# An adaLN block with a gated delta rule: balanced join products, q norms from turned rows, and a table position for every side step

## The chip, the cores and the metric

The kernel runs on one core of one Trainium2 chip, in one launch. The metric is device time in microseconds of the whole program. A profiled execution is one run with the hardware profiler on; its "span" reaches from the first to the last instruction that the profile shows. In the text TensorE is PE, VectorE is DVE, ScalarE is ACT, GpSimd is POOL and SyncE, which issues nearly all DMAs, is SP. Each of them works through its own instructions in order and waits, where it must, on semaphores that another engine or a DMA raises.

## What is computed

Input `x` has 8 sequences of 512 rows and 256 channels. Modulation vectors come from `silu(c) @ wmod`. Then, in float32 throughout:

```python
h = layernorm(x) * (1 + ca) + sa
x = x + ga * attn(h)
h = layernorm(x) * (1 + cb) + sb
x = x + gb * ffn(h)          # top 2 of 6 experts, chosen per sequence

def attn(h):                 # 16 key heads, 32 value heads, all of width 128
    qkvz = h @ W_qkvz.T      # q, k, v, z
    q, k, v = silu(conv4(qkv))              # causal depthwise convolution, 4 taps
    beta, g = sigmoid(b), -exp(A_log) * softplus(a + dt_bias)
    # chunked delta rule
    A = -strict_tril((k * beta) @ k.T * decay)
    T = inverse(I - A)       # a triangular inverse for each chunk
    u = T @ (v * beta), ...  # v_new = u - (T k beta exp(g)) @ state
    out = (q exp(g)) @ state + tril(q @ k.T * decay) @ v_new
    state = state * exp(g_last) + (k exp(g_last - g)).T @ v_new
    return (rmsnorm(out) * norm_weight * silu(z)) @ W_out.T
```

`q` and `k` are divided by their norms over the 128 channels. The kernel works in chunks of 128 rows (4 per sequence) where the reference has 64; the mathematics is the same.

## The kernel before

**Pairs and turns.** The work is cut into 128 "pairs": 8 sequences times 16 key heads; a pair holds one key head and its two value heads. For each pair, over a hundred small steps (`step[name]`) are defined, each of which issues the instructions of one engine, sometimes several DMAs. A table `PLACE` gives every step a position. The step of pair n stands at `n * 1000 + PLACE[name]`; `TURN = 1000`. All steps of all pairs are sorted by this position and issued in that order, under `tc.manual_schedule()`, so the order on each engine is the order of the table. Since positions run from -600 to 13049, about 14 pairs are in flight at once, and in the middle of the run each turn issues the same sequence of steps, one of every name, each of another pair. A position says only in which order things are queued: an engine starts the next instruction as soon as its semaphores allow.

**What the steps are.** `pk`, `pq`, `pv0`, `pv1`, `pz0`, `pz1` project (PE, 128x512 outputs); `ck`, `ck1` to `ck3` and the like are the four taps of the convolution (the first on ACT, three on DVE); `sk`, `sq`, `sv0`, `sv1` are the SiLUs (ACT). `kt` turns k on PE into PSUM, `kn0` and `kn1` take squares with row sums of it (ACT), `kp` the root (POOL), `ks` the scalars (DVE). For q, `qq` squares on POOL in channel-by-row form, `ssq` sums over channels by four matmuls against a column of ones, `qc` copies the result (DVE), `qp` and `qs` finish. `kk0`, `kk1` are the products of keys with keys and queries, `dr0`, `dr1`, `de` the decays (ACT), `mt*`, `qk*` (DVE) and `md*`, `sd*` (POOL) mask and decay them. `mo`, `so*`, `ko`, `qo` write to DRAM; `in0`, `in1`, `jd`, `jc` bring things back in another layout.

**The triangular inverse.** For every fourth pair, 32x32 diagonal blocks of four pairs lie one matrix to a lane, and DVE inverts them in twenty parts that are spread over four turns as `lane0` to `lane4` (lines 831 to 916). The blocks are then joined to 64 and to 128 by PE products: `jw` makes the first product of both joins (lines 968 and 970, outputs in PSUM partitions 0 to 63 and 64 to 127), ACT copies (`jwa`, `jwb`), `jy` makes the second product (lines 990, 991 and 997), ACT copies (`jya`, `jyb`). The join to 64 belongs to pair n, the join to 128 to pair n - 1. Line 991 makes the transposed form of the 64-join that the 128-join needs as its `x6`.

**The chunk steps.** `pk1`..`pq3` multiply by the state, `r*` (DVE) the residual, `u*` (PE) applies the inverse, `wd*` (DVE) and `w*` (ACT) scale, `ds*` (PE) and `st*` (DVE) make the next state, `i*` (PE) and `o*` (DVE) the output, `sq0`..`sq3` (ACT), `rm` (DVE), `rp`, `sc0`, `sc1` (POOL) the RMS norm, `ot*`, `gt*`, `op*` turn, gate and project out.

**PSUM.** All PE outputs but the sums of the projection out come from one pool of six banks. A PE step that takes a bank waits for the last reader of that bank's earlier content, so an ACT or DVE step that is late can hold up a PE step that has nothing else to do with it.

**Side steps.** Once per sequence come `before_attention` (layer norm, gates, decay sums: 29 steps) and `after_attention` (second norm, choice of experts, loads of their weights, FFN: 45 steps). In the kernel before they stand at a regular distance: the lines that place them are

```python
order.append((at + 20 * TURN, lambda b=b: gates(b)))
if b:
    order.append((at - 5 * TURN - TURN // 2, lambda b=b: load_rows(b)))
    for k, fn in enumerate(before_attention(b)):
        order.append((at - 5 * TURN + 3 * TURN * k // 20, fn))
for k, fn in enumerate(after_attention(b)):
    order.append((at + 28 * TURN + TURN // 2 + TURN * k // 5, fn))
```

with `at = 16 * b * TURN`.

Of the kernel before, what the change touches and what calls it, by code (L numbers as in the profile page):

```python
# [22 lines left out]

TURN = 1000
PLACE = {
    "wk": -600, "pk": -547, "ck": -460, "ck1": -393, "pq": -382, "gb": -377, "ck2": -361, "ck3": -303,
    "cq": -282, "sk": -168, "cq1": -109, "cq2": -103, "cq3": -38, "kt": 50, "sq": 83, "kn0": 89,
    "kra": 221, "kn1": 225, "qq": 280, "kp": 290, "dr1": 291, "kk0": 294, "ssq": 311, "dr0": 320,
    "ks": 329, "kk1": 372, "qk0": 385, "mt0": 394, "qc": 397, "qk1": 406, "mt1": 433, "de": 469,
    "qo": 501, "md0": 502, "ko": 556, "sd0": 641, "so0": 675, "md1": 708, "mo": 716, "sd1": 729,  # L30
    "so1": 1144, "qp": 1244, "qs": 1781, "tl": 4319, "lane0": 4503, "lane1": 4583, "lane2": 4627,
    "lane3": 4678, "lane4": 4704, "wv": 6947, "lx": 7757, "ly": 7904, "pv1": 7948, "cv1": 8064,
    "pv0": 8175, "cv11": 8201, "cv12": 8276, "cv13": 8314, "cv0": 8316, "sv1": 8357, "cv01": 8398,
    "cv02": 8454, "jd": 8458, "cv03": 8508, "jw": 8589, "sv0": 8603, "jwa": 8629, "jwb": 8688,
    "jy": 8744, "jya": 8835, "jyb": 8900, "vt0": 8977, "jc": 8982, "vt1": 9015, "vr0": 9101,
    "vr1": 9119, "in0": 9637, "in1": 9670, "u0": 9932, "wd0": 9966, "w0": 10062, "ds0": 10127,
    "st0": 10137, "pk1": 10297, "r1": 10350, "i0": 10386, "u1": 10392, "o0": 10432, "wd1": 10450,
    "ds1": 10495, "w1": 10549, "st1": 10613, "pq1": 10683, "pk2": 10700, "tm1": 10719, "r2": 10724,
    "pq2": 10765, "tm2": 10863, "u2": 10907, "i1": 10925, "wd2": 10939, "o1": 10972, "w2": 11006,
    "ds2": 11017, "st2": 11136, "sq0": 11170, "i2": 11200, "wz": 11202, "o2": 11296, "pk3": 11322,  # L40
    "r3": 11353, "u3": 11396, "pq3": 11462, "w3": 11518, "sq1": 11538, "i3": 11541, "tm3": 11554,
    "sq2": 11574, "o3": 11619, "sq3": 11714, "pz1": 11731, "sz1": 11785, "pz0": 11813, "rm": 11878,
    "rp": 11940, "sz0": 11994, "sc0": 12039, "sc1": 12051, "ot0": 12154, "ot1": 12163, "gt0": 12243,
    "gt1": 12277, "op0": 12366, "op1": 12477, "xa0": 12865, "xa1": 13049,
# [31 lines left out]
def adaln_block(  # L76
# [91 lines left out]
    def norm_transposed(b, shift, scale, name):  # L168
# [42 lines left out]
        steps = [*[lambda c=c: stats(c) for c in range(NC)], deviations, roots]  # L211
        for kt in range(NKT):
            steps += [
                lambda kt=kt: scaled(kt, 0), lambda kt=kt: scaled(kt, 1),
                lambda kt=kt: turned(kt), lambda kt=kt: shifted(kt),
            ]
        return steps

    def before_attention(b):
# [81 lines left out]
        def g_leaves():  # L301
            d["gfar"] = gfar.tile([P, P], F32, name=f"gfar_{b}", tag="gfar")
            nc.sync.dma_start(d["gfar"], t["gt"])

        return [
            *norm_transposed(b, 0, 2, "a"), betas, sigmoid, biased, soft, soft_exp, ratio,
            lambda: series(15, 13, 11, 9), lambda: series(7, 5, 3), soft_end,
            decay_sums, decay_exp, decay_rest, g_turned, g_copy, g_leaves,
        ]

    def after_attention(b):
# [46 lines left out]
        def experts():  # L358
            s1 = f["s1"] = tiny("w1", [P, NKT, 2 * DFF])
            s2 = f["s2"] = tiny("w2", [P, NF, DM])  # L360
            v1 = f["v1"] = tiny("b1", [P, NF])
            v2 = f["v2"] = tiny("b2", [P, 2, DM])
            for k in range(2):
                e = nc.sync.value_load(f["ix"][0:1, k : k + 1], min_val=0, max_val=NE - 1)
                nc.sync.dma_start(
                    s1[:, :, k * DFF : (k + 1) * DFF],
                    w1[bass.ds(e, 1)].rearrange("e (kt p) f -> p (e kt) f", p=P),
                )
                for at, t, q, n in hidden_parts(k, 0, DFF):
                    nc.sync.dma_start(  # L370
                        s2[q : q + n, t, :], w2[bass.ds(e, 1), at : at + n, :].rearrange("e p m -> (e p) m")
                    )
                for half in range(2):
                    for at, t, q, n in hidden_parts(k, half * FP, FP):
                        at -= half * FP
                        nc.sync.dma_start(
                            v1[q : q + n, t : t + 1],
                            b1[bass.ds(e, 1), at : at + n, half : half + 1].rearrange(
                                "e p t -> p (e t)"
                            ),  # L380
                        )
                nc.sync.dma_start(
                    v2[:, k, :], b2[bass.ds(e, 1)].to_broadcast([P, DM])
                )
# [14 lines left out]
        def hidden(i, t):  # L399
            ps = f["ps", t] = bank(f"f1_{b}_{i}_{t}")  # L400
            for kt in range(NKT):
                mm(
                    ps[: MF[t], : 2 * P], f["s1"][:, kt, t * P : t * P + MF[t]],
                    d["hb"][:, kt, 2 * i * P : (2 * i + 2) * P], start=kt == 0, stop=kt == NKT - 1,
                )

        def gelu(i, t):
            if t == 0:
                f["hid"] = row.tile([P, NF, 2 * P], F32, name=f"hid_{b}_{i}", tag="hid", bufs=1)
            nc.scalar.activation(  # L410
                f["hid"][: MF[t], t, :], f["ps", t][: MF[t], : 2 * P], AF.Gelu,
                bias=f["v1"][: MF[t], t : t + 1],
            )

        def result(i):
            ps = f["f2"] = bank(f"f2_{b}_{i}")
            for c2 in range(2):
                for t in range(NF):
                    mm(
                        ps[:, c2 * DM : (c2 + 1) * DM], f["hid"][: MF[t], t, c2 * P : (c2 + 1) * P],  # L420
# [3 lines left out]
        def result_rows(i):  # L424
            o = f["o"] = row.tile([P, 2, DM], F32, name=f"of_{b}_{i}", tag="of", bufs=1)
            nc.vector.tensor_add(
                o, f["f2"].rearrange("p (c m) -> p c m", m=DM), bc_mid(f["v2"][:, 0, :], 2)
            )

        def result_gated(i):  # L430
            nc.vector.tensor_mul(f["o"], f["o"], bc_mid(d["gb"], 2))

        def result_added(i):
            nc.vector.tensor_add(f["o"], f["o"], d["x"][:, 2 * i : 2 * i + 2, :])

        def result_leaves(i):
            nc.sync.dma_start(
                out[b, 2 * i * P : (2 * i + 2) * P, :].rearrange("(c p) d -> p c d", p=P), f["o"]
            )

        steps = [
            *norm_transposed(b, 4, 6, "b"), column_sums, logits, choose, choice_exp, shares, spread,
            spread_copy, experts, weigh,
        ]
        for i in range(2):
            for t in range(NF):
                steps.append(lambda i=i, t=t: hidden(i, t))
                steps.append(lambda i=i, t=t: gelu(i, t))
            for fn in (result, result_rows, result_gated, result_added, result_leaves):
                steps.append(lambda i=i, fn=fn: fn(i))  # L450
# [50 lines left out]
    for step in before_attention(0):  # L501
        step()
# [10 lines left out]
    with ExitStack() as st:  # L513
# [162 lines left out]
        def q_squares(n, d):  # L676
            q = d["kqa"][:, :, 1, :]
            d["sq"] = w1b.tile([P, NC, P], F32, name=f"sq_{n}", tag="sq")
            nc.gpsimd.tensor_tensor(d["sq"], q, q, ALU.mult)  # L679

        def q_sums(n, d):
            ps = d["ssq"] = bank(f"ssq_{n}")
            for c in range(NC):
                mm(ps[:, c : c + 1], d["sq"][:, c, :], ones[:, 0:1], start=True, stop=True)  # L684

        def q_copy(n, d):
            d["nrm"] = sm.tile([P, NC], F32, name=f"nrm_{n}", tag="nrm")
            nc.vector.tensor_copy(d["nrm"], d["ssq"][:, :NC])  # L688
# [106 lines left out]
        add("qq", q_squares)  # L795
        add("ssq", q_sums)
        add("qc", q_copy)
# [184 lines left out]
        def join_y(n, d):  # L982
# [3 lines left out]
            for u in range(8):  # L986
                us = slice(64 * u, 64 * u + 64)
                if n < NPAIR:
                    y = d["y"]
                    mm(p5[:64, us], w5[:, u, :], halves(y[:, u, :]), start=True, stop=True)  # L990
                    mm(
                        p5[64:, 32 * u : 32 * u + 32], y[:, u, 0:64], w5[:, u, 0:32],
                        start=True, stop=True,
                    )
                if n > 0:
                    y = its[n - 1]["y"]
                    mm(p6[:64, us], w6[:, u, :], y[:, u, 64:128], start=True, stop=True)

        def join_y_128(n, d):
            if n > 0:  # L1000
                nc.scalar.copy(its[n - 1]["y"][0:64, :, 64:128], of_u(d["p6"], 64)[0:64])

        def join_y_64(n, d):
            if n < NPAIR:
                y, v = d["y"], of_u(d["p5"], 64)
                nc.scalar.copy(x6[32:64, :, 0:32], of_u(d["p5"], 32)[96:128])
# [3 lines left out]
        joins = ("jw", "jwa", "jwb", "jy", "jya", "jyb")  # L1010
        for name, fn in zip(joins, (join_w, join_w_128, join_w_64, join_y, join_y_128, join_y_64)):
# [261 lines left out]
        for b in range(NB):  # L1273
            at = HK * b * TURN
            order.append((at + 20 * TURN, lambda b=b: gates(b)))
            if b:
                order.append((at - 5 * TURN - TURN // 2, lambda b=b: load_rows(b)))
# [50 lines left out]
```

## Time and profile before

| what | value |
|---|---|
| median of 3 runs | 4172.03 us (4171.61 to 4175.54) |
| the profiled execution's own time | 4170.47 us |
| span of the profiled execution | 4168.8 us |
| mean granted PE clock | 0.984 |
| PE / DVE / ACT / POOL busy | 4006.1 / 3521.5 / 3180.3 / 1619.1 us |
| PE instructions | 27184 |

The profiled execution's time is 1.7 us over its span and 1.6 us under the median. A float32 matmul or its weight load appears as two PE instructions where the program has one; a transpose appears once. A busy time counts an instruction from its start to its modelled end, so PE's busy share includes the overlap of one matmul's end with the next one's start; distances from start to start say what an instruction costs in a stream. The profile's granted clock is 0.9 or more of full speed in all but the first slices of the span.

### The profile page before, as it was taken

The page shows a single profiled execution, that of the slowest core. Times are in us where ns is not written, and L with a number is a line of the kernel's source. Part 1 is how long each engine was busy: PE and PEld are TensorE (multiplying, and loading weights), DVE is VectorE, ACT ScalarE, POOL GpSimd, SP SyncE. Part 2 cuts the span into 40 slices and gives each one's busy share as a digit, 9 for nine tenths or more (in the row PEclk, how much of TensorE's full clock was granted, in tenths as well). Part 3 has the DMA queues.
Part 4 walks back from the last instruction along what each step waited for, and adds up shares of the span by engine and source line. Part 5 has one row for each costly group of instructions (what it writes and reads, how often), then busy time and mean ns, then how long its engine had stood idle before and what let it go on. Part 6 is the DMA issues. An engine that isn't in the chain of part 4 may idle for free.

```text
span 4168.8 us, 84578 instructions
## 1 busy us (share of the span) xinstructions
PE 4006.1 (96%) x27184; PEld 2968.0 (71%) x27184; DVE 3521.5 (84%) x7974; ACT 3180.3 (76%) x8946; POOL 1619.1 (39%) x1576
## 2 busy tenths in 40 slices
PE   6689999999999999999999999999999999999997
PEld 4467777777777777777777777777777777777776
DVE  4888888988899888898889888889888988889754
ACT  4578777778777787778877788777887778777663
POOL 4443444334443434433343434443434434444211
PEclk7799999999999999999999999999999999999999
DMA  4676666666666666656667566665667666666441
GB/s 122 158 191 169 175 174 185 171 165 171 176 174 162 177 166 180 180 147 175 176 176 182 160 166 175 175 176 166 167 169 183 169 165 175 172 169 178 131 115 49
DMA packets 1101605, 689.37 MB, mean 165 GB/s; under 512 B 667368, under 2 KB 964712, under 8 KB 1101168
## 3 DMA queue, kind: packets, MB, share of 16 engines
q1 hardware_dynamic: 1100352, 682.14, 61.3%
q8 instruction: 222, 3.64, 0.4%
q14 instruction: 215, 1.76, 0.1%
q10 hardware_dynamic: 816, 1.84, 0.1%
HBM read 435.68 MB, written 248.00 MB: 164 GB/s over the span
## 4 chain that ended last, share of the span: by engine, by line
PE 83%; DVE 10%; ACT 2%; DMA 2%; SPq 2%; issue 1%; POOL 0%; POOLq 0%; ACTq 0%; DVEq 0%
PE prv L590 10%; PE acc L1232 9%; PE prz L1187 9%; PE kk L722 6%; PE in L1140 5%; PE prk L590 5%; PE u L1096 5%; PE prq L590 4%; PE pk L1066 4%; PE pq L1071 4%; PE dst L1118 4%; PE ot L1213 3%; PE ssq L684 3%; PE vt L1022 2%; PE w L968 2%; PE py L990 2%
## 5 line engine op out<-in xcount | busy, mean ns | idle before, releaser
L1203 POOL TENSOR_TENSOR msq<-msq,mhalf 128x8 f32<-128x8 f32 x128 | 210.6, 1646 | 1216.2 <-DVE msq L1197 1216.2
L745 POOL TENSOR_TENSOR mta<-mta,dca 128x512 f32<-128x512 f32 x256 | 339.4, 1326 | 657.1 <-DVE nrm L688 391.1
L606 DVE SCALAR_TENSOR_TENSOR cvv<-prv,cw,cvv 128x511 f32<-128x511 f32 (+2 forms) x768 | 566.6, 738 | 0.4
L1111 ACT ACTIVATE w<-u,kept 128x128 f32<-128x128 f32 x1024 | 317.8, 365 | 317.9 <-PE u L1096 198.4
L590 PE MATMUL prv<-ha,wv 128*128 128x512 f32 x1024 | 488.2, 599 | 11.7 <-ACT jk L652 6.0
L1232 PE MATMUL acc<-wo,z 128*128 128x256 f32 x2048 | 484.1, 379 | 0.5 <-DVE z L1219 0.5
L1187 PE MATMUL prz<-ha,wz 128*128 128x512 f32 x1024 | 481.6, 593 | 2.8 <-DVE nrm L695 2.8
L1232 PEld LDWEIGHTS acc<-wo,z 128*128 128x128 f32 x2048 | 388.8, 190 | 61.0 <-issue 7.7
L752 POOL TENSOR_TENSOR dca<-qkm,dca 128x256 f32<-128x256 f32 x512 | 399.5, 801 | 20.1
L1140 PEld LDWEIGHTS in<-w,s 128*128 128x128 f32 x2048 | 298.8, 191 | 73.4 <-issue 39.0
L1103 DVE TENSOR_TENSOR wd<-u,kept 128x256 f32<-128x256 f32 x384 | 160.3, 418 | 218.0 <-PE u L1096 217.2
L707 ACT ACTIVATE dca<-gb,G 128x128 f32<-128x128 f32 x1024 | 328.3, 413 | 4.8 <-DMA sfar<-dca 4.8
L1162 ACT ACTIVATE jo<-o 128x128 f32<-128x128 f32 x1024 | 310.3, 313 | 6.6 <-DVE o L1153 3.2
L1140 PE MATMUL in<-w,s 128*128 128x128 f32 x2048 | 312.5, 275 | 0.0
L606 DVE SCALAR_TENSOR_TENSOR cvk<-prk,cw,cvk 128x511 f32<-128x511 f32 (+2 forms) x384 | 283.3, 738 | 15.9 <-ACT cvk L602 15.6
L1187 PEld LDWEIGHTS prz<-ha,wz 128*128 128x128 f32 x1024 | 193.9, 190 | 140.0 <-issue 123.1
L606 DVE SCALAR_TENSOR_TENSOR cvq<-prq,cw,cvq 128x511 f32<-128x511 f32 (+2 forms) x384 | 285.4, 743 | 4.9
L722 PE MATMUL kk<-kqa 128*128 128x256 f32 x1024 | 279.4, 397 | 6.0 <-ACT kqa L619 6.0
L679 POOL TENSOR_TENSOR sq<-kqa 128x512 f32<-128x512 f32 x128 | 133.2, 1041 | 377.8 <-ACT kqa L619 377.8
L590 PEld LDWEIGHTS prv<-ha,wv 128*128 128x128 f32 x1024 | 176.0, 192 | 140.3 <-issue 124.3
L1029 DVE TENSOR_TENSOR vr<-vt,kept 128x512 f32<-128x512 f32 x256 | 164.6, 685 | 128.8 <-PE vt L1022 128.8
L990 PEld LDWEIGHTS py<-y,w 128*64 128x64 f32 x2048 | 200.8, 138 | 100.2 <-issue 75.8
(211 smaller groups left out, 11143.6 us busy)
## 6 DMA issues: line engine op xcount, KB each, us to landing
gb<-gfar SPq DMA_DIRECT2D x128, 512.0 KB, 9.2
qfar<-kqa SPq DMA_DIRECT2D x128, 512.0 KB, 2.7
sfar<-dca SPq DMA_DIRECT2D x256, 256.0 KB, 3.6
s<-sfar SPq DMA_DIRECT2D x256, 256.0 KB, 4.5
wk<-in_dram SPq DMA_DIRECT2D x256, 128.0 KB, 3.4
kfar<-kra SPq DMA_DIRECT2D x128, 256.0 KB, 3.1
wv<-in_dram SPq DMA_DIRECT2D x128, 256.0 KB, 3.6
kq<-qfar SPq DMA_DIRECT2D x128, 256.0 KB, 3.7
```

Of the source, the lines that this page charges most:

```text
L590: mm(ps, d[wname][:, kt, j * P : (j + 1) * P], hT[:, kt, :], start=kt == 0, stop=kt == NKT - 1,)
L606: nc.vector.scalar_tensor_tensor(a[:, s:], ps[:, : SEQ - s], cw[:, ch, 3 - s : 4 - s], a[:, s:], ALU.mult, ALU.add)
L707: nc.scalar.activation(dc[:, c, h, :], d["gb"][:, 2 * gr + c, h * P : (h + 1) * P], AF.Relu, bias=rows[b]["G"][:, 2 * gr + c, k : k + 1], ...
L722: mm(ps[:, c2 * 2 * P : (c2 + 1) * 2 * P], d["kqa"][:, c, 0, :], d["kqa"][:, c].rearrange("p k i -> p (k i)"), start=True, stop=True,)
L745: nc.gpsimd.tensor_tensor(mt, mt, d["dc", gr].rearrange("p c h i -> p (c h) i"), ALU.mult)
L752: nc.gpsimd.tensor_tensor(dc, bc_mid(d["qkm", gr][:, c, :], 2), dc, ALU.mult)
L990: mm(p5[:64, us], w5[:, u, :], halves(y[:, u, :]), start=True, stop=True)
L1111: nc.scalar.activation(w[:, h, :], d["u", c][:, h * P : (h + 1) * P], AF.Copy, scale=d["br2"][:, c, h : h + 1],)
L1140: mm(ps[:, h * P : (h + 1) * P], d["s", c, h], d["w", c][:, h, :], start=True, stop=True,)
L1162: nc.scalar.activation(junk, d["o", c // 2][:, c % 2, h, :], AF.Square, accum_out=d["msq"][:, c, h : h + 1],)
L1187: mm(ps, d["wz"][:, kt, h * P : (h + 1) * P], rows[n // HK]["ha"][:, kt, :], start=kt == 0, stop=kt == NKT - 1,)
L1232: mm(ps[:, k * DM : (k + 1) * DM], d["z", h][:, c * P : (c + 1) * P], d["wo"][:, h, :], start=False, stop=p == HK - 1 and k == 1 and h == 1,)
```

## The change

It does four things.

1. In `jy`, line 991 is dropped, and the product of the 128-join (line 997) is written to PSUM partitions 64 to 127 instead of 0 to 63, so that two products per block remain, one for each column half. The transposed form is made by a new DVE step `jx` that transposes 32x32 blocks out of PSUM into `x6`; ACT's copy into `x6` is dropped from `jyb`.
2. The norm of q: `qq` (POOL), `ssq` (PE) and `qc` (DVE) are dropped. `qt` turns q on PE into PSUM, as `kt` does for k, and `qn0`, `qn1` take squares with row sums of it on ACT.
3. Every side step has a position of its own in `PLACE`. The loads of the experts are cut into `e0`, `e1` (weights) and `eb0`, `eb1` (biases), and each of the four reads the chosen index into a register again.
4. The whole table has new positions.

```diff
 PLACE = {
-    "wk": -600, "pk": -547, "ck": -460, "ck1": -393, "pq": -382, "gb": -377, "ck2": -361, "ck3": -303,
-    "cq": -282, "sk": -168, "cq1": -109, "cq2": -103, "cq3": -38, "kt": 50, "sq": 83, "kn0": 89,
-    "kra": 221, "kn1": 225, "qq": 280, "kp": 290, "dr1": 291, "kk0": 294, "ssq": 311, "dr0": 320,
-    "ks": 329, "kk1": 372, "qk0": 385, "mt0": 394, "qc": 397, "qk1": 406, "mt1": 433, "de": 469,
-    "qo": 501, "md0": 502, "ko": 556, "sd0": 641, "so0": 675, "md1": 708, "mo": 716, "sd1": 729,
-    "so1": 1144, "qp": 1244, "qs": 1781, "tl": 4319, "lane0": 4503, "lane1": 4583, "lane2": 4627,
-    "lane3": 4678, "lane4": 4704, "wv": 6947, "lx": 7757, "ly": 7904, "pv1": 7948, "cv1": 8064,
-    "pv0": 8175, "cv11": 8201, "cv12": 8276, "cv13": 8314, "cv0": 8316, "sv1": 8357, "cv01": 8398,
-    "cv02": 8454, "jd": 8458, "cv03": 8508, "jw": 8589, "sv0": 8603, "jwa": 8629, "jwb": 8688,
-    "jy": 8744, "jya": 8835, "jyb": 8900, "vt0": 8977, "jc": 8982, "vt1": 9015, "vr0": 9101,
-    "vr1": 9119, "in0": 9637, "in1": 9670, "u0": 9932, "wd0": 9966, "w0": 10062, "ds0": 10127,
...
+    "wk": -600, "gb": -466, "pk": -424, "ck": -411, "ck1": -321, "ck2": -300, "pq": -221, "ck3": -167,
+    "cq": -166, "sk": -82, "cq1": -70, "cq2": -24, "kt": 38, "dr0": 59, "cq3": 89, "kn0": 148,
+    "kra": 174, "sq": 176, "kn1": 211, "dr1": 273, "kp": 291, "ks": 333, "de": 354, "kk0": 357,
+    "qt": 366, "qk0": 382, "qn0": 386, "mt0": 401, "qn1": 472, "kk1": 524, "mt1": 566, "qo": 586,
+    "qk1": 587, "ko": 740, "md0": 769, "sd0": 802, "so0": 893, "md1": 1031, "sd1": 1090, "mo": 1100,
+    "so1": 1247, "qp": 1492, "qs": 1954, "tl": 4393, "lane0": 4459, "lane1": 4600, "lane2": 4619,
+    "lane3": 4636, "lane4": 4682, "wv": 7823, "pv1": 7944, "lx": 7957, "cv1": 8036, "ly": 8055,
+    "cv11": 8091, "cv12": 8119, "pv0": 8152, "cv13": 8257, "cv0": 8290, "cv01": 8359, "cv02": 8433,
+    "sv1": 8490, "jd": 8495, "cv03": 8508, "jw": 8527, "jwa": 8556, "jwb": 8558, "sv0": 8616,
+    "jy": 8694, "vt0": 8717, "jya": 8743, "vr0": 8746, "jyb": 8772, "jx": 8798, "vt1": 8836,
+    "vr1": 8847, "jc": 9415, "in0": 9794, "u0": 9844, "lr": 9871, "an0": 9920, "wd0": 9927, "w0": 9948,
+    "ds0": 9958, "st0": 9999, "an1": 10001, "pk1": 10149, "r1": 10223, "i0": 10243, "an2": 10249,
+    "o0": 10313, "u1": 10338, "wd1": 10371, "in1": 10373, "w1": 10409, "ds1": 10607, "st1": 10640,
+    "sq0": 10725, "pk2": 10736, "r2": 10766, "pq1": 10845, "pq2": 10856, "tm1": 10888, "u2": 10908,
+    "tm2": 10919, "i1": 10922, "wd2": 10941, "an3": 10949, "o1": 10953, "adv": 10979, "w2": 10992,
+    "ds2": 11039, "st2": 11095, "art": 11115, "ax00": 11131, "pk3": 11210, "ax01": 11229, "r3": 11267,
+    "i2": 11284, "sq1": 11301, "o2": 11331, "u3": 11374, "w3": 11406, "pq3": 11431, "at0": 11454,
...
+    "gt0": 12285, "gt1": 12299, "ba": 12384, "op0": 12394, "bsig": 12430, "bdt": 12480, "sp0": 12569,
...
+    "sp5": 14087, "gs": 14623, "gx": 14631, "gr": 14689, "gt": 14987, "gc": 14993, "gl": 15461,
...
+    "bt1": 31080, "bh1": 31169, "hs": 31212, "lg": 31392, "ch": 31469, "e0": 31839, "cx": 32156,
+    "e1": 32796, "cs": 33250, "cb": 33385, "cc": 33509, "eb0": 34071, "eb1": 34473, "f00": 34539,
+    "g00": 34663, "f01": 35929, "we": 35937, "g01": 36160, "f02": 36376, "g02": 36457, "re0": 36889,
+    "rr0": 37114, "f10": 38444, "f11": 38497, "g10": 38523, "g11": 38706, "rg0": 39072, "ra0": 39372,
+    "f12": 39375, "g12": 39432, "rl0": 39955, "re1": 40300, "rr1": 40414, "rg1": 41117, "ra1": 41246,
+    "rl1": 43977,
 }
...
-        def q_squares(n, d):
-            q = d["kqa"][:, :, 1, :]
-            d["sq"] = w1b.tile([P, NC, P], F32, name=f"sq_{n}", tag="sq")
-            nc.gpsimd.tensor_tensor(d["sq"], q, q, ALU.mult)
-
-        def q_sums(n, d):
-            ps = d["ssq"] = bank(f"ssq_{n}")
+        def q_turned(n, d):
+            ps = d["qt"] = bank(f"qt_{n}")
             for c in range(NC):
-                mm(ps[:, c : c + 1], d["sq"][:, c, :], ones[:, 0:1], start=True, stop=True)
-
-        def q_copy(n, d):
-            d["nrm"] = sm.tile([P, NC], F32, name=f"nrm_{n}", tag="nrm")
-            nc.vector.tensor_copy(d["nrm"], d["ssq"][:, :NC])
+                nc.tensor.transpose(ps[:, c * P : (c + 1) * P], d["kqa"][:, c, 1, :], ident)
+
+        def q_squares(n, d, i):
+            if i == 0:
+                d["nrm"] = sm.tile([P, NC], F32, name=f"nrm_{n}", tag="nrm")
+            for c in (2 * i, 2 * i + 1):
+                junk = w2b.tile([P, P], F32, name=f"jq_{n}_{c}", tag="jk")
+                nc.scalar.activation(
+                    junk, d["qt"][:, c * P : (c + 1) * P], AF.Square,
+                    accum_out=d["nrm"][:, c : c + 1],
+                )
...
                     mm(p5[:64, us], w5[:, u, :], halves(y[:, u, :]), start=True, stop=True)
-                    mm(
-                        p5[64:, 32 * u : 32 * u + 32], y[:, u, 0:64], w5[:, u, 0:32],
-                        start=True, stop=True,
-                    )
                 if n > 0:
                     y = its[n - 1]["y"]
-                    mm(p6[:64, us], w6[:, u, :], y[:, u, 64:128], start=True, stop=True)
+                    mm(p6[64:, us], w6[:, u, :], y[:, u, 64:128], start=True, stop=True)
 
         def join_y_128(n, d):
             if n > 0:
-                nc.scalar.copy(its[n - 1]["y"][0:64, :, 64:128], of_u(d["p6"], 64)[0:64])
+                nc.scalar.copy(its[n - 1]["y"][0:64, :, 64:128], of_u(d["p6"], 64)[64:128])
 
         def join_y_64(n, d):
             if n < NPAIR:
                 y, v = d["y"], of_u(d["p5"], 64)
-                nc.scalar.copy(x6[32:64, :, 0:32], of_u(d["p5"], 32)[96:128])
                 nc.scalar.copy(y[0:32, :, 32:64], v[0:32, :, 0:32])
                 nc.scalar.copy(y[64:96, :, 96:128], v[32:64, :, 32:64])
 
+        def join_x_64(n, d):
+
+            if n < NPAIR:
+                nc.vector.transpose(x6[32:64, :, 0:32], of_u(d["p5"], 64)[0:32, :, 0:32])
...
         for b in range(NB):
             at = HK * b * TURN
-            order.append((at + 20 * TURN, lambda b=b: gates(b)))
-            if b:
-                order.append((at - 5 * TURN - TURN // 2, lambda b=b: load_rows(b)))
-                for k, fn in enumerate(before_attention(b)):
-                    order.append((at - 5 * TURN + 3 * TURN * k // 20, fn))
-            for k, fn in enumerate(after_attention(b)):
-                order.append((at + 28 * TURN + TURN // 2 + TURN * k // 5, fn))
+
+            side = {"ga": lambda b=b: gates(b)} | after_attention(b)
+            if b + 1 < NB:
+                side |= {"lr": lambda b=b: load_rows(b + 1)} | before_attention(b + 1)
+            order += [(at + PLACE[name], fn) for name, fn in side.items()]
```

## The prediction

> **What bounds the kernel now.** I read the page first, then the table of stretches, the groups by line, and the timelines of one turn.
>
> ```profile
> PE 4006.1 (96%) x27184; PEld 2968.0 (71%) x27184; DVE 3521.5 (84%) x7974; ACT 3180.3 (76%) x8946; POOL 1619.1 (39%) x1576
> ```
>
> PE is busy 96% of the span. Whether it is the limit is told by stretches: first one sequence (16 turns, from one late `prv` to the next), then four turns without side steps. Columns: window, length, then busy time and instructions of PE, weight loads, DVE, ACT, POOL, then granted clock, DMA share, GB/s.
>
> ```profile
> 1766.30:2267.37 501.07, 492.40 (x3394) 366.40 (x3394) 438.74 (x996) 398.23 (x1120) 200.67 (x194) 1.00 0.66 172
> 2559.49:2589.00 29.51, 29.51 (x209) 22.00 (x207) 26.70 (x58) 23.26 (x71) 12.35 (x12) 1.00 0.64 169
> 2589.00:2618.50 29.50, 29.50 (x208) 21.99 (x207) 25.28 (x54) 23.14 (x71) 12.02 (x12) 1.00 0.58 164
> 2618.50:2648.00 29.50, 29.50 (x208) 21.99 (x207) 24.73 (x54) 23.14 (x70) 12.88 (x12) 1.00 0.65 202
> 2648.00:2677.50 29.50, 29.50 (x208) 21.99 (x207) 26.37 (x66) 23.25 (x70) 12.06 (x12) 1.00 0.67 178
> ```
>
> A plain turn takes 29.50 us and PE never pauses in it: PE is the bound, and what leaves PE leaves the turn, until DVE stops it. DVE needs 24.7 to 26.7 us (the lanes differ over four turns), and its largest idle times are waits for PE:
>
> ```profile
> DVE wd L1103 <- PE u L1096: 217.2, 115, 5.3
> DVE vr L1029 <- PE vt L1022: 128.8, 104, 2.2
> ```
>
> A sequence takes 501.07, which is 29.1 us over 16 x 29.50: the side steps and what they disturb. Their PE work alone is about 16.6 us (48 FFN matmul instructions at 0.215, and the small ones), so some 12 us are lost around them.
>
> **Part 1, the joins.** Columns of a group: busy us, mean ns, idle before it.
>
> ```profile
> L990 PE MATMUL py<-y,w 128*64 128x64 f32 x2048 | 252.0, 226 | 3.4 <-ACT w L980 3.4
> L997 PE MATMUL py<-y,w 128*64 128x64 f32 x2048 | 246.0, 223 | 2.3 <-ACT tmp L1087 2.3
> L991 PE MATMUL py<-w,y 128*64 128x32 f32 x2048 | 240.6, 233 | 0.0
> L968 PE MATMUL w<-x,m 128*64 128x64 f32 x2048 | 147.9, 225 | 0.0
> L970 PE MATMUL w<-x,m 128*64 128x64 f32 x2048 | 146.6, 225 | 0.5
> ```
>
> The mean says nothing, the spacing does. In `jy` (from 2578.63, `pq` after it at 2580.64: 2.01 us) one block's instructions follow at 0.117, since L990 and L997 share the lower column half. In `jw`, L968 and L970 lie in different halves, start within 0.01 us of each other, and a pair takes 0.058. With L997 in the upper half, `jy` is a second `jw`: 16 x 0.058 less, **-0.94 us of PE a turn**. ACT loses the `x6` copy (0.37); `jya` now reads the upper partitions and writes the lower ones, as the dropped `x6` copy did across partitions, and I leave it at its 0.58. DVE gains `jx`, which no row shows. It lies between the 128x128 copy out of PSUM (0.28) and a 128x512 operation (0.68); nearest is the 128x256 copy (0.42, 0.35 to the next start), which I take. `jx` waits for ACT's second `jyb` copy, with `ck3`, `vr1`, `wd0` queued behind it; by the layout below `jyb` is done 2 us before.
>
> **Part 2, the norms of q.**
>
> ```profile
> L684 PE MATMUL ssq<-ones,sq 128*128 128x1 f32 x1024 | 128.1, 246 | 0.1
> L632 PE MATMUL kt<-ident,kqa 128*128 128x128 f32 x512 | 79.2, 278 | 44.9 <-ACT kqa L619 44.9
> 2592.46 0.95 PE L684 MATMUL ssq<-ones,sq 128*128 128x1 f32 x8
> 2593.27 0.68 PE L1066 MATMUL pk<-st,kq 128*128 128x256 f32 x2
> 2587.25 0.60 PE L632 MATMUL kt<-ident,kqa 128*128 128x128 f32 x4
> 2587.69 0.60 PE L1118 MATMUL dst<-wd,kr 128*128 128x256 f32 x2
> ```
>
> Eight instructions in 0.81 go, four like `kt` in 0.44 come (fp32 transposes appear once, matmuls twice): **about -0.40 of PE** with the rounding of starts. POOL loses 1.04, DVE 0.07. ACT gains four squares with read-outs, 0.52 for two where `kn0` stands: +1.05, less 0.37 above, 23.2 to 23.9 of 28 us: covered. If that cover were gone, `pk` would wait for `qn1`, whose bank it takes; by the layout `qn1` ends 2 us before.
>
> **Part 3, can DVE follow?** PE alone would turn in 29.50 - 0.94 - 0.40 = 28.16. I laid one turn of the new table out with the spacings of the timeline. DVE must wait for `pk3` before `r3`, and PE's `u2` takes the bank that `ck3` reads last. Between them PE does eleven steps at 0.44, five at 0.43, `kk0` and `kk1` (1.72), `op0`, `pk`, `op1`, `pq` (6.88) and both joins with their edges (2.4): 17.99. DVE does `r3` 0.56, `gt` 1.34, `o` 0.68, `ks` 0.96, five taps 3.28 and the last 0.74, `wd1` 0.34, `qk` 0.67, `mt` 1.20, `st1` 0.52, `o3` 0.34, `vr0` 0.60, `r2` 0.52, `jx` 0.35: 12.09, and 0.28 for crossing over and back. That leaves 5.6 us for lanes, 5.8 as my list is 0.2 short of the turn. The lanes of the four turns took 7.47, 5.93, 5.38 and 7.42: 1.67, 0.13, 0 and 1.62 too long, **0.85 us on average given back**. Elsewhere (`u2` to `pk3`, 9.9 of PE against 7.3 of DVE) DVE has 2.6 to spare. PE's `pk2` also waits some 0.45 for `jya`, inside the same stretch, so this is not added. Turn: 28.16 + 0.85 = 29.0.
>
> One rule speaks against the change.
>
> ```profile
> 2628.45 1.79 DVE L906 TENSOR_TENSOR prl<-wt,yl 128x1024 f32<-128x1024 f32 x1
> 2633.45 1.21 DVE L906 TENSOR_TENSOR prl<-wt,yl 128x1024 f32<-128x1024 f32 x1
> 2629.23 2.28 POOL L752 TENSOR_TENSOR dca<-qkm,dca 128x256 f32<-128x256 f32 x2
> ```
>
> The same lane product takes 1.21 alone and 1.79 beside POOL's products, of which two take 2.28 instead of 1.41. The Trainium skill ("SBUF — State Buffer", "Who interferes with whom") says that a VectorE instruction with two SBUF inputs and a GpSimd one that reads SBUF exclude each other, the second one waiting until the first is done. `mt1` moves from 433, before the lanes, to 566, behind `lane0`, so `md1` and `sd1` (1.28 and 1.41) now run beside `lane1` to `lane3`. By the rows, the lanes hold about 0.65 of blocking a turn already, and I keep that (0.85 back); by the rule each of the six POOL instructions can hold DVE once, and 0.4 more makes it 1.15 (turn 29.3). With no blocking it would be 0.5 (28.7).
>
> **Part 4, side steps.** In the new table most of DVE's (`sp2` to `sp5`, `ax`, `bx00` to `bx10`, `we`, `hs`) fall at 868 to 258 of a turn, where DVE has room, and PE's (`ba`, `f00`, `f02`, `f10`, `f11`, `f12`, `re1`) at 300 to 540, where PE waits. Of 16.6 us of PE work some 10.5 fall there, half of it free: 5 remain, 6 elsewhere, 4 of DVE work in the tight stretch, 2 of rest: 17 instead of 29. Loads are queued closer to their readers than before: `jc` 112 positions (3 us) ahead of the `jw` that reads it instead of 607, `jd` 32 instead of 131, `lr` 49 ahead of `an0` instead of 500. That costs nothing if SP runs ahead of the table: its turn has some 17 us of issues, and it stops only where `gb` waits for `dr1`, at 273, and `so1` for `sd1`, at about 700; so `jc` and `jd` leave at about 730 of the turn before, 20 us before `jw` (they land in 2 to 4), and `lr` some 14 us before `an0` (it lands in 4.6). Were SP not ahead, `jw` would stand 2 to 3 us a turn and PE with it, which is the whole gain twice over; `gl` waits for `gc` and holds SP some 8 us once a sequence, with `jd` behind it, which still has 8 us. Register reads are doubled (four for two) on SP only; if that room is gone, it is a few us a sequence. The finer cost of all this I bound by 12 us either way per sequence.
>
> **The sum.** A sequence: 16 x 29.0 + 17 = 481, 20 less. Between 222 and 3769 us there are 7.08 such: -142. The last 400 us hold about eight full turns: -4. In the first nine turns nothing of the joins runs, while ACT has 1.05 more each: +8. So 4170.5 - 138 = 4032 for the profiled execution; the median of the runs stands 1.6 above it: **4035 us**.
>
> **The rivals.**
>
> *PE stays the bound.* For it: the sums of part 3 are good to half a us, and DVE has room over the whole turn (26 of 28.2). Against: the two long lane turns. Then -1.34 x 128 = -171 and half of the 12 us lost around side steps (-44): 3955, or 4003 if `pk2`'s wait for `jya` counts: 3980.
>
> *Slower: POOL holds the lanes.* If blocking at the lanes grows by more than 1.5 us a turn, the stretch of DVE is too long in all four turns and the gain is gone (16 x 30.4 + 14 = 501). POOL has 5.4 us of products a turn to do it with; at 2.2 us it gives 31.1 a turn, +11 a sequence, 4250. Against it: in the trace a POOL product blocks a lane once, for 0.6 to 1.1.
>
> *It doesn't do what it says.* If the halves do not run together in `jy` (same weights' side, or `jx` late), only the 0.40 goes; then the stretch has 0.94 more room for DVE, the turn is 29.4, and the side steps are still better placed: 4080.
>
> **How the numbers follow.** DVE-limited in two of four turns, 4035: 0.58, its own range 3985 to 4095. PE-bound, 3980: 0.22. Slower by blocking: 0.12. No join gain: 0.08. 3970 to 4130 leaves out a third of the second case and the third. A measurement of this kernel tells about 0.2%, 8 us. Faster 0.86, same 0.02, slower 0.12.
>
> **What would show it.** Right: L990's and L997's counterparts start within 0.01 us and `jy` takes about 1.1; PE has 0.5 to 1.7 us of idle before `u2` or `pv1` in two of four turns, ended by DVE (`ck3`, `vr1`); turns of 28.2 to 29.8; PE busy lower by some 170. Wrong: even turns of 28.2 (PE-bound), lane products mostly over 1.7 us (blocking), or PE idle that ends at a DMA or at ACT.

## The result, and the profile after

The changed kernel takes **4212.75 us** (median of 4 runs, 4211.64 to 4214.97) against 4171.82 before (median of 4): a ratio of 1.0099, 95% interval 1.0082 to 1.0117. It is 41 us (1.0%) slower where 137 us less was forecast. The profiled execution has a span of 4209.9 us.

The page of the kernel after: busy times, then the chain of work that ended last, by engine.

```profile
PE 3916.9 (93%) x24624; PEld 2770.8 (66%) x24624; DVE 3688.3 (88%) x7974; ACT 3249.9 (77%) x9843; POOL 1559.4 (37%) x1448
PE 43%; DVE 43%; ACT 5%; issue 4%; DMA 3%; SPq 1%; POOL 1%; DVEq 0%; POOLq 0%; ACTq 0%
```

The same chain of the kernel before:

```profile
PE 83%; DVE 10%; ACT 2%; DMA 2%; SPq 2%; issue 1%; POOL 0%; POOLq 0%; ACTq 0%; DVEq 0%
```

PE lost 89 us of busy time and three points of its share. In the chain DVE now has as much of the time as PE. DVE gained 167 us of busy time, though the only instruction it gained, `jx`, has 56 us. The rest is the lanes': the same number of instructions takes 984 us in all where it took 867.

Stretches of after: one sequence, then a cycle of four turns without side steps.

```profile
1571.16:2075.70 504.54, 484.03 (x3074) 343.29 (x3073) 460.62 (x996) 406.65 (x1231) 194.20 (x178) 0.99 0.64 170
412.70:444.87 32.17, 30.10 (x188) 21.41 (x187) 28.14 (x66) 23.66 (x75) 11.23 (x11) 0.95 0.72 190
444.87:476.55 31.68, 28.98 (x188) 20.37 (x186) 28.51 (x58) 23.77 (x75) 11.69 (x11) 1.00 0.60 161
476.55:506.00 29.45, 28.94 (x187) 20.38 (x186) 26.38 (x54) 23.77 (x75) 11.89 (x11) 1.00 0.61 162
506.00:534.28 28.28, 28.28 (x187) 20.30 (x186) 25.22 (x54) 23.77 (x75) 12.97 (x11) 1.00 0.57 173
```

The even 29.50 is gone. The shortest turn is 28.28, all of it PE: that is what the operations alone were to give (28.16). The two turns with the long lanes take 32.17 and 31.68, and the mean is 30.4, the very turn at which the forecast's slower rival breaks even.

What the new operations cost, groups of after:

```profile
L1018 PE MATMUL py<-y,w 128*64 128x64 f32 x2048 | 148.3, 226 | 5.9 <-issue 3.9 <-ACT w L1008 2.0
L1021 PE MATMUL py<-y,w 128*64 128x64 f32 x2048 | 147.0, 226 | 3.3 <-ACT hb L219 3.3
L706 PE MATMUL qt<-ident,kqa 128*128 128x128 f32 x512 | 80.5, 282 | 0.0
L1036 DVE STREAM_TRANSPOSE x<-py 32x256 f32<-32x256 f32 x128 | 56.3, 440 | 5.7 <-ACT y L1031 1.8
```

`jy` is now a second `jw` (147 and 148 us busy, as `jw` had), `qt` costs what `kt` costs, and `jx` takes 0.44 us and stands 1.8 us in all for ACT's copy. Nothing of the gain is lost here.

PE's two largest new waits for DVE in after (us in total, times, longest):

```profile
PE pk L1094 <- DVE st L1158: 103.2, 66, 2.7
PE u L1124 <- DVE vr L1057: 17.5, 38, 0.7
```

`pk2` waits for `st1` about 2.1 us in two turns of four. `st1` stands on DVE behind `lane1`, `lane2` and `lane3`. The timeline of the first long turn around it (start, duration, and in brackets the idle time before):

```profile
428.02 0.41 DVE L769 TENSOR_TENSOR qkm<-kk,tri_le 128x256 f32<-128x256 f32 x1
...
428.25 1.26 POOL L773 TENSOR_TENSOR mta<-mta,dca 128x512 f32<-128x512 f32 x1 [1.78 <-DVE mta L761]
...
428.35 1.36 DVE L876 TENSOR_TENSOR prl<-yl,tl 128x100 f32<-128x100 f32 x1
...
429.59 1.60 POOL L780 TENSOR_TENSOR dca<-qkm,dca 128x256 f32<-128x256 f32 x2
...
433.61 0.60 DVE L1158 SCALAR_TENSOR_TENSOR st<-st,ex,dst 128x128 f32<-128x128 f32 x2
...
434.36 0.67 PE L1094 MATMUL pk<-st,kq 128*128 128x256 f32 x2 [2.07 <-DVE st L1158]
```

POOL's `md1` starts as soon as DVE's `mt1` is done; DVE has `qk1` left and then meets it with a lane product that has two inputs in SBUF. The product takes 1.36 us where it takes 0.33 without POOL's products (below); for about the first microsecond it stands for `md1`.

### The profile page after: what moved, and what is told of

Same layout as the page of the kernel before. It is cut to its first block, busy times and chain, and to the rows that moved or that the text cites. A ratio compares the mean times of both kernels' runs of the same rounds, so it can differ in the third digit from the quotient of the medians.

```text
span 4209.9 us, 80074 instructions
## 1 busy us (share of the span) xinstructions
PE 3916.9 (93%) x24624; PEld 2770.8 (66%) x24624; DVE 3688.3 (88%) x7974; ACT 3249.9 (77%) x9843; POOL 1559.4 (37%) x1448
## 4 chain that ended last, share of the span: by engine, by line
PE 43%; DVE 43%; ACT 5%; issue 4%; DMA 3%; SPq 1%; POOL 1%; DVEq 0%; POOLq 0%; ACTq 0%
PE prz L1215 8%; PE prv L617 8%; DVE cvv L633 4%; DVE cvk L633 4%; PE u L1124 3%; DVE mta L761 3%; DVE prl L920 3%; PE acc L1260 3%; PE pk L1094 3%; PE in L1168 3%; PE dst L1146 2%; DVE prl L876 2%; DVE z L1247 2%; PE prq L617 2%; DVE prl L911 2%
## 5 line engine op out<-in xcount | busy, mean ns | idle before, releaser
L773 POOL TENSOR_TENSOR mta<-mta,dca 128x512 f32<-128x512 f32 x256 | 327.7, 1280 | 820.9 <-ACT jq L713 596.6
L780 POOL TENSOR_TENSOR dca<-qkm,dca 128x256 f32<-128x256 f32 x512 | 478.1, 953 | 20.1
L1260 PEld LDWEIGHTS acc<-wo,z 128*128 128x128 f32 x2048 | 372.4, 191 | 49.8 <-issue 7.6
L1139 ACT ACTIVATE w<-u,kept 128x128 f32<-128x128 f32 x1024 | 305.4, 376 | 97.8 <-DVE wd L1131 72.9
L1105 DVE SCALAR_TENSOR_TENSOR r<-pk,neg,vr 128x128 f32<-128x128 f32 x768 | 232.3, 344 | 164.1 <-PE pk L1094 163.3
L1115 ACT ACTIVATE tmp<-pq,ex 128x128 f32<-128x128 f32 x768 | 238.8, 366 | 173.4 <-PE pq L1099 173.0
L685 POOL TENSOR_TENSOR kept<-kept,half 128x4 f32<-128x4 f32 x128 | 129.2, 1009 | 570.1 <-ACT jk L679 494.8
L1094 PE MATMUL pk<-st,kq 128*128 128x256 f32 x768 | 239.2, 394 | 104.8 <-DVE st L1158 103.2
L1094 PEld LDWEIGHTS pk<-st,kq 128*128 128x128 f32 x768 | 136.7, 192 | 244.8 <-issue 206.6
L1168 PE MATMUL in<-w,s 128*128 128x128 f32 x2048 | 296.0, 278 | 0.0
```

Source lines behind the costliest of these rows:

```text
L773: nc.gpsimd.tensor_tensor(mt, mt, d["dc", gr].rearrange("p c h i -> p (c h) i"), ALU.mult)
L780: nc.gpsimd.tensor_tensor(dc, bc_mid(d["qkm", gr][:, c, :], 2), dc, ALU.mult)
L1094: mm(ps[:, : 2 * P], d["kq", c][:, 0, :], st, start=True, stop=True)
L1139: nc.scalar.activation(w[:, h, :], d["u", c][:, h * P : (h + 1) * P], AF.Copy, scale=d["br2"][:, c, h : h + 1],)
L1168: mm(ps[:, h * P : (h + 1) * P], d["s", c, h], d["w", c][:, h, :], start=True, stop=True,)
L1260: mm(ps[:, k * DM : (k + 1) * DM], d["z", h][:, c * P : (c + 1) * P], d["wo"][:, h, :], start=False, stop=p == HK - 1 and k == 1 and h == 1,)
```

## The experiments

T1: the new order sets POOL's products against the lanes, in a stretch of DVE that has no slack, and every us of blocking beyond the room becomes a us of turn. T2: the order does it without blocking. T3: the new operations cost what they save. The letters in the forecasts below are these.

**The operations without the order.** The old table, with only the new joins and norms:

```diff
 # before
+    "jx": 8910,          # new joins
-    "qq": 280, "ssq": 311, "qc": 397,
+    "qt": 311, "qn0": 470, "qn1": 471,      # new q norms
```

> The kernel before with its own table of positions (main steps and side steps), and only the new joins (jx at 8910) and the new q norms (qt 311, qn0 470, qn1 471). T1 (lane products held by POOL in the new order) and T2 (the new order packs too much DVE work between r3 and ck3, whoever holds it) both say that the two changes of operations are sound and that the order alone lost their gain: turns of 28.2 to 28.8, about 4000 to 4050 us. T3 (the new joins or norms cost as much as they save, on DVE or ACT): 4160 to 4215.

Measured: 4051.25 us, ratio to before 0.9713 (0.9684 to 0.9741). The four plain turns of one cycle:

```profile
515.95:544.43 28.48, 28.48 (x187) 20.71 (x186) 26.97 (x67) 23.76 (x76) 11.01 (x11) 1.00 0.76 206
544.43:572.59 28.16, 28.16 (x188) 20.48 (x186) 27.31 (x59) 23.40 (x76) 11.20 (x11) 1.00 0.68 189
572.59:600.71 28.12, 28.12 (x187) 20.57 (x186) 25.27 (x55) 23.92 (x76) 12.15 (x12) 1.00 0.65 173
600.71:628.84 28.13, 28.13 (x188) 20.57 (x187) 25.34 (x55) 23.66 (x76) 11.84 (x11) 1.00 0.69 188
```

PE fills every turn at 28.1 to 28.5, though DVE is as busy as before. T3 falls: parts 1 and 2 save 1.38 us a turn.

**The joins alone**, on the old table:

> The kernel before with only the new joins (jx at 8910). Part 1 as costed (0.94 us of PE a turn, jx covered): turns of 28.56, some 115 us less, 4050 to 4070 us. If jx or the altered copies take something back: 4080 to 4130. If the halves did not run together: 4165 to 4180.

Measured: 4093.50 us (0.9815, 0.9787 to 0.9844). Plain turns are 28.58 in nearly all cases, 0.92 less, as costed; by subtraction the q norms, which were not run alone, account for the other 0.46. The total missed its band: a sequence fell by 10 us instead of 14.7. The turns with side steps keep part of it back, one of 34.05 even growing to 34.75. What limits those turns is open.

**The order without the operations.** The new table with the old joins and norms:

```diff
 # after
-    "qt": 366, "qn0": 386, "qn1": 472, "jx": 8798,
+    "qq": 335, "ssq": 366, "qc": 403,       # and the old joins
```

> The new table with the old operations: after with the old joins and the old q norms (qq at 335, ssq at 366, qc at 403, no jx). T1: the order alone is what costs; the two long turns are set by DVE and the lanes as in after (31.3 to 32.2, or 0.4 less as jx is gone), the two short ones by PE at 29.5, so about 30.6 a turn, 4210 to 4250 us, slower than before. T3 (the loss needs the new operations, the order being harmless): PE's 29.5 sets all four turns, 4130 to 4180.

Measured: 4233.52 us (1.0151, 1.0121 to 1.0180), as T1 has it. Plain turns 31.0, 31.3, 29.6 and 29.5: the short ones stand at PE's old turn, the long ones where after has them, a little lower without `jx`. With this the four corners are known:

| median us | old operations | new operations |
|---|---|---|
| old order | 4172 | 4051 |
| new order | 4234 | 4213 |

The operations are worth 121 us in the old order and 21 in the new one. The new order costs 62 with the old operations and 162 with the new: in the long turns PE had less to do, but DVE set their length.

**Without POOL's products**, in the new order and in the old:

```diff
-            nc.gpsimd.tensor_tensor(mt, mt, d["dc", gr]..., ALU.mult)      # md0, md1
-                nc.gpsimd.tensor_tensor(dc, bc_mid(d["qkm", gr]...), dc, ALU.mult)  # sd0, sd1
+            pass
```

> The kernel after with POOL's products md0, md1, sd0, sd1 left out (it leaves the decay factor out of M and of the scores). T1: lane products at their unblocked times (512-wide 0.67 instead of 1.37 to 1.72), lanes 7 us instead of 9 in the two long turns, no wait of pk2 for st1; all four turns 28.3 to 29.3, about 4010 to 4040 us. T2 (order alone, blocking unimportant): long turns stay above 31, 4170 to 4200.

> e3_both with POOL's md and sd products left out (it leaves the decay factor out of M and of the scores), as e4_nopool does for the new order, where it was worth 172 us. T1: in the old order PE sets the turn at 28.1 to 28.5 and the blocked lanes are covered, so at most 25 us to gain, 4025 to 4050. Rival (POOL's blocking costs its time in any order): 3900 to 3980.

Measured: 4040.45 us in the new order, 172 less than after; 4011.07 in the old, 40 less than 4051. Two groups of lane products and one of lane copies, first of before, then of after, then of the new order without POOL's products:

```profile
L883 DVE TENSOR_TENSOR prl<-wt,yl 128x512 f32<-128x512 f32 x64 | 66.4, 1038 | 0.0
L848 DVE TENSOR_TENSOR prl<-yl,tl 128x100 f32<-128x100 f32 x32 | 13.1, 408 | 0.0
L885 DVE COPY yl<-xl 128x64 f32<-128x64 f32 x64 | 27.9, 436 | 2.2
```

```profile
L911 DVE TENSOR_TENSOR prl<-wt,yl 128x512 f32<-128x512 f32 x64 | 95.7, 1496 | 0.0
L876 DVE TENSOR_TENSOR prl<-yl,tl 128x100 f32<-128x100 f32 x32 | 38.9, 1216 | 0.0
L913 DVE COPY yl<-xl 128x64 f32<-128x64 f32 x64 | 37.1, 579 | 2.2
```

```profile
L906 DVE TENSOR_TENSOR prl<-wt,yl 128x512 f32<-128x512 f32 x64 | 43.6, 681 | 0.0
L871 DVE TENSOR_TENSOR prl<-yl,tl 128x100 f32<-128x100 f32 x32 | 10.5, 328 | 0.0
L908 DVE COPY yl<-xl 128x64 f32<-128x64 f32 x64 | 13.8, 216 | 2.2
```

The instructions and their order are the same on DVE; 1.50 becomes 0.68 and 1.22 becomes 0.33. Copies are held too, although they have one input: 0.58 becomes 0.22 here, and the smaller copy from `tl` to `yl` (128x4) goes from 0.67 to 0.16. These two copies make up about 40 of the 195 us that all lanes of after take more than those of this kernel. The turns of this kernel:

```profile
518.04:547.20 29.16, 28.75 (x187) 20.32 (x186) 25.71 (x66) 23.79 (x75) 5.66 (x5) 1.00 0.76 205
547.20:576.38 29.18, 29.01 (x187) 20.35 (x186) 26.01 (x58) 23.79 (x75) 5.66 (x5) 1.00 0.70 174
576.38:604.81 28.43, 28.37 (x188) 20.23 (x187) 25.36 (x54) 23.79 (x75) 5.66 (x5) 1.00 0.63 168
604.81:632.99 28.18, 28.18 (x187) 20.43 (x186) 24.53 (x54) 23.68 (x75) 5.66 (x5) 1.00 0.63 180
```

Their mean is 28.74: the forecast's figure for "no blocking" was 28.7. T2 falls as the main cause; order alone is 0.6 us a turn. Without POOL's products the new order costs 29 us (4040 to 4011), with them 162. In the old order plain turns become 28.12 throughout, which is about 1.6 us of the 4 that a sequence fell; the rest came in turns with side steps, and nearly half of the 40 us in the first 28 turns. 40 us is more than T1 allowed (25) and far from the rival's 70 and more: the lanes of the old order lose 95 us to POOL's products (882 to 787) and the program loses 40, where in the new order the lanes lose 195 and the program 172.

What is left out also takes SP's waits for these products with it (119 us in after). That is not where the gain comes from: PE's largest wait for a load, that of `wv`, was 7.2 us in after and is 11.1 here.

**The masks back ahead of the lanes**, all else as in after:

```diff
-    "kk1": 524, "mt1": 566, "qk1": 587,
+    "kk1": 359, "qk1": 403, "mt1": 434,
```

> The kernel after with kk1, qk1 and mt1 at 359, 403 and 434 instead of 524, 587 and 566, so ahead of the lanes as before, which lets POOL start md1 and sd1 sooner, while the rest of the new order stays. T1: about 1 us of blocking less in the two long turns, 0.5 us a turn, 8 a sequence, about 4150 us. T2: the stretch holds the same DVE work, so within 10 us of 4213.

Measured: 4156.00 us (0.9965, 0.9949 to 0.9981), near T1's 4150: 57 of the 162 come back with three positions. POOL's four products now run back to back; the lanes take 8.4 and 8.0 us in the long turns instead of 8.9 and 9.3, and these turns 31.0 and 30.4.

**The mirror: the masks behind `lane0` in the old order.**

```diff
 # e3_both
-    "kk1": 372, "qk1": 406, "mt1": 433,
+    "kk1": 524, "mt1": 566, "qk1": 587,
```

> The mirror of e6_masks: e3_both (old order, new operations, 4051 us) with only kk1, qk1 and mt1 at the new table's places (524, 587, 566, behind lane0). T1: this move alone sets POOL's md1 and sd1 against the lanes; about 1.3 us more of lanes in two of four turns, of which the old order covers a part, turns of 28.4 to 29.2 on average, 4070 to 4140 us. T2 (the place of these steps matters only inside the new order): 4045 to 4060.

Measured: 4171.56 us, slower than either side expected, and for another reason. Lanes were not blocked more (852 us in all, against 882 in the kernel it was made from). DVE's largest wait, and PE's:

```profile
DVE mta L734 <- PE kk L723: 271.8, 124, 4.6
PE prq L590 <- ACT w L975: 62.0, 90, 0.9
```

DVE stands at `mt1` for PE's `kk1`, 2.2 us a turn, with the lanes queued behind, so POOL and lanes moved together. PE itself waits for ACT ahead of `prq`, where it waited 4.1 us in all before the move, and plain turns take 28.9. How the one wait leads to the other is open. Of blocking the run says only that the masks' late place does not make the collision by itself in the old order.

**The lanes out of the stretch.**

```diff
 # after
-    "lane3": 4636, "lane4": 4682,
+    "lane3": 4942, "lane4": 4943,
```

> The kernel after with lane3 and lane4 moved from 4636 and 4682 to 4942 and 4943, so behind st1, vr0, r2 and ck3 where DVE has idle time and POOL has no md or sd product. T1 and T2 both: the stretch r3 to ck3 loses 2.4 us in the long turns, the turns of 32.2 and 31.7 become 29 to 29.5, about 4040 us. T3 (another cause: ACT, SP's loads, the joins): the long turns stay, 4190 to 4215.

Measured: 4200.46 us. The turn of 31.7 did fall to 29.8 and the last two to 28.1, but the first of the four rose to 34 to 37. SP's waits, and PE's wait in such a turn:

```profile
SPq L957 <- DVE xl L940: 326.9, 32, 16.4
```

```profile
3200.57 3.75 PE L617 MATMUL prv<-ha,wv 128*128 128x512 f32 x4 [4.31 <-DMA wv<-in_dram]
```

The last lane of a group now ends later, SP stands at `lx` for it up to 16.4 us (93.2 in all in after, 9.3 at most), and `gb`, `wz` and `wv`, queued behind `lx`, leave late. PE waits 45.7 us in all for `wv`, and 49.6 for what comes back of `lx`. So the expectation was right for the stretch and missed what a later lane holds up on SP. No theory is decided by this run; it shows that the lanes cannot be moved there without holding up SP.

**`st1` ahead of the lanes**, to take away PE's largest new wait:

```diff
 # after
-    "ds1": 10607, "st1": 10640,
+    "ds1": 10592, "st1": 10598,
```

> The kernel after with ds1 and st1 at 592 and 598 instead of 607 and 640, so that st1 stands ahead of lane1 to lane3 and pk2 need not wait for it (the largest new wait of PE: 103 us in all). T1: the wait only shows where the DVE stretch from r3 to ck3 is felt first; its sum is the same, PE waits later, for vr0 or ck3: within 25 us of 4213. Rival (the wait of pk2 is itself the loss): about 100 us less, 4110 to 4130.

Measured: 4264.24 us (1.0225, 1.0195 to 1.0254), slower still. The waits of one long turn, DVE's and then PE's:

```profile
3751.28 0.61 DVE L1158 SCALAR_TENSOR_TENSOR st<-st,ex,dst 128x128 f32<-128x128 f32 x2 [1.37 <-PE dst L1146]
```

```profile
3759.86 0.71 PE L1124 MATMUL u<-vr,y 128*128 128x128 f32 x4 [1.72 <-DVE vr L1057]
```

`pk2` no longer waits. PE waits for `vr0` instead (141.5 us in all, 17.5 in after), and DVE now stands 1.1 to 1.4 us for `ds1` with the later lanes behind it. The rival falls: taking the wait of `pk2` away gains nothing, and PE waits one step later. T1's own band was missed too; it did not count the new wait of DVE.

**The side steps' new places in the old order.**

```diff
 # e3_both
-    # side steps at 3/20 and 1/5 of a turn from each other
+    # side steps at after's own positions
```

> Old main order, new operations, and after's own positions for the side steps (e3_both with only the side steps moved). If the side steps' new places are good by themselves (17 to 18 us a sequence instead of the 32 of e3_both): 3940 to 3970 us. If they are good only with the gaps of the new main order: 4030 to 4060 or slower.

Measured: 4077.20 us (0.9776, 0.9748 to 0.9804), 26 slower than with the regular spacing. Side steps cost 38 us a sequence there, 33 with the regular spacing, and about 19 in after. So the places are not good by themselves. That they need the new order's gaps, in which PE waits anyway, fits the two orders, but no run shows it.

**`jx` ahead of ACT's copies**, in the fastest kernel so far:

```diff
 # e3_both
-    "jx": 8910,
+    "jx": 8834,
```

> e3_both with jx at 8834 instead of 8910, ahead of ACT's copies jya and jyb, not behind them. In e3_both jx stood 68.6 us in all waiting for ACT's copy, in turns with side steps, and PE some 40 us for jx. If that wait is a loss of its own: 4005 to 4035 us. If ACT's copies now wait for jx, or are what PE waits for next: 4040 to 4055. If DVE stands at jx for PE's jy with work queued behind it: 4060 to 4100.

Measured: 4050.66 us (0.9707, 0.9691 to 0.9723), no different from 4051.25. A wait of DVE in the one, of PE in the other:

```profile
DVE x L1009 <- ACT y L1004: 68.6, 50, 3.5
```

```profile
PE vt L1023 <- ACT w L1112: 27.9, 12, 3.8
```

DVE's wait for ACT is gone, and PE now waits for ACT itself, 27.9 us where it waited 26.8 for `jx`: in those turns ACT is late. Both kernels beat the kernel before by 2.9%, and after by 3.8% (4051 to 4213).

## Why the prediction was wrong, by its own steps

**Parts 1 and 2 held.** PE alone turns in 28.12 where 28.16 was summed, `jx` takes 0.44 for 0.42, and its wait for ACT was 1.8 us in all.

**Part 3: the room was right, the lanes were not.** The forecast had a turn as 28.16, plus what the lanes take beyond 5.8 us. Here are the lanes' times by turn, put into that formula; they are the summed durations of DVE's instructions that write `prl`, `yl`, `xl` or `wt`:

| turn of the cycle | lanes after | formula | measured | lanes without POOL's products | formula | measured | lanes, masks back | formula | measured |
|---|---|---|---|---|---|---|---|---|---|
| 1 | 8.93 | 31.29 | 32.17 | 6.52 | 28.88 | 29.16 | 8.38 | 30.74 | 31.02 |
| 2 | 9.31 | 31.67 | 31.68 | 6.83 | 29.19 | 29.18 | 8.01 | 30.37 | 30.37 |
| 3 | 7.11 | 29.47 | 29.45 | 6.07 | 28.43 | 28.43 | 6.79 | 29.15 | 29.14 |
| 4 | 5.93 | 28.29 | 28.28 | 5.24 | 28.16 | 28.18 | 5.77 | 28.16 | 28.19 |

Nine of twelve turns come out within 0.03 us; the first of the cycle is 0.3 longer in each kernel, for a reason not found here, and the rest of that turn of after is the clock (below). So the layout of the stretch and its room were sound for this order.

The term that failed is the blocking that the lanes carry. Without POOL's products the four turns have 24.66 us of lanes. Before had 27.36, so 0.68 of blocking a turn: the forecast's 0.65. After has 31.28, so **1.66 a turn, where the forecast kept 0.65**. With the masks back ahead of the lanes it is 1.07, so the place of these three steps makes more than half of the growth. By the formula the growth of 0.98 is 1.0 us of turn. Another 0.2 is the forecast's reading of the lanes by their starts (5.93 and 7.42 in two of the turns, where the durations sum to 6.33 and 7.75), and 0.2 is the first turn of the cycle, most of it the clock. These 1.4 us, 16 times in each of 7.08 sequences, are 158 of the 178 us by which the forecast missed; counted by a cycle in which the clock did not fall they are 141.

**The rule that spoke against it was right and was weighed too lightly.** The Trainium skill ("SBUF — State Buffer", "Who interferes with whom") has a VectorE instruction with two SBUF inputs and a GpSimd one that reads SBUF exclude each other for a whole instruction. The rows agree: the product of 0.33 took 1.36 beside a POOL product of 1.26, the one of 0.68 took 1.37 and 1.72. Reductions over the same lanes, one input, kept their time; the copies did not, and the forecast, which went by two inputs, had no term for them. It priced the rule at 0.4 of blocking more than the rows and then took the rows, which were measured in an order where most of the collisions did not occur. Even the rule's price, 0.65 and 0.4, was 0.6 us too low on average: in the long turns the lanes lost 2.4 and 2.5 us.

**The rival "POOL holds the lanes" is what happened**, with its break-even turn of 30.4 hit, and its own threshold wrong: it asked for 1.5 us more a turn, and 0.98 was enough, because the 0.4 of the two smaller terms above came on top. That the turn came out at just 30.4 is chance. The sign that was to show it, lane products mostly over 1.7 us, was set too high as well; 1.36 to 1.72 did it.

**Part 4 held in its number, in part by luck.** Side steps cost about 19 us a sequence where 17 was forecast and 29 were paid before. But they did so beside turns longer than the forecast's, in which PE waits more: in the same order without POOL's products, with a turn of 28.74 near the forecast's 29.0, a sequence takes 483 and the side steps 23. Loads were in time (PE stood 7.2 us in all for `wv`). That SP runs ahead was right here, and one lane moved too late ends it.

**PE's busy time** fell by 89, not 170; with the same operations in the old order it fell by 155. In the first long turn of after PE is busy 30.1 us for 28.2 of work, some of it at a lower clock. The forecast's sign "PE idle before `u2` or `pv1`, ended by DVE" was right in kind and wrong in place: it came at `pk2`, whose `st1` is the first step behind the lanes that PE needs.

## What to carry to other kernels

When work leaves the engine that bounds a kernel, sum the next engine's work between the two points where they meet, with the durations that its instructions will have in the new order. How long a lane product takes depends on what runs beside it (0.33 or 1.36 us here). Where POOL's products are moved, the old row's mean is not the new one's, and the time without them should be measured, or bounded from both sides. A change of order and a change of operations belong in separate runs: here the one was worth -121 us and the other cost 162 on top of it, and together they looked like a change that does nearly nothing.

## What the hardware showed that was not expected

After the pause of 2.07 us in the first long turn the granted clock fell. Stretches of that turn of after, columns as above, the clock third from the end:

```profile
432.00:434.30 2.30, 0.29 (x3) 0.05 (x1) 2.27 (x6) 1.05 (x3) 0.00 (x0) 1.00 1.08 388
434.30:436.00 1.70, 1.64 (x5) 0.99 (x6) 1.70 (x3) 0.69 (x4) 0.00 (x0) 0.87 0.85 254
436.00:438.00 2.00, 2.00 (x5) 0.85 (x4) 2.00 (x5) 0.18 (x1) 0.00 (x0) 0.50 0.42 77
438.00:440.00 2.00, 2.00 (x11) 1.91 (x11) 1.94 (x5) 0.74 (x2) 0.00 (x0) 0.76 0.74 188
```

`prq`, whose four instructions take 1.88 us, took 2.92. Four turns later the same place paused 2.05 us at a clock of 1.00 throughout, and the turn took 31.55 instead of 32.17: the wait costs its own length, and sometimes 0.6 us more. Between 300 and 4100 us of after PE paused for more than 2 us 33 times; 19 times a stretch of 3.41 us at half the clock followed, 14 times none. By an estimate from the two turns (19 times 0.6) this is some 11 us in all. Before had four such pauses there and no such stretch. The Trainium skill ("TensorE: Matmul & The Clock Gate", "What's actually happening") lets the clock drop after an idle window of about 3.4 us; here pauses of 2.06 and 2.07 were enough in two turns and one of 2.05 was not in another, so a pause shorter than the window can do it. What decides between them no run here shows.
